# Fourth layer of a graph network: gathered rows in one ring of two chunks, refilled four tiles at a time

## The chip, the cores and the metric

One core of one Trainium2 chip. The time is that of one launch of the whole kernel on the device, in microseconds (us), median over runs. TensorE (PE) multiplies matrices, VectorE (DVE) and ScalarE (ACT) work on elements, GpSimd (POOL) here mostly issues DMAs whose addresses come from an index list, SyncE (SP) issues the other DMAs.

## The reference, cut to what matters

12 500 nodes with 32 features each, 400 000 edges sorted by destination. Four layers, each `x = x + layer(relu(layernorm(x)))`. The change is in the fourth:

```python
# edge_sh = edge_attr_4 (E, 4), edge_scalars = edge_attr_8 (E, 8); E = 400000, MUL = 8
h = relu(edge_scalars @ (fc_w1 / sqrt(8))) * SQRT2               # (E, 256)
w = (h @ (fc_w2 / sqrt(256))).reshape(E, 4, MUL, MUL)            # weights of each edge
x = node_features[edge_src]                                      # one gathered row of 32 an edge
s1, v1 = x[:, :MUL], x[:, MUL:].reshape(E, MUL, 3)
s2, v2 = edge_sh[:, 0], edge_sh[:, 1:4]
out_s = A_SCALAR * (einsum('eu,euw->ew', s1 * s2[:, None], w[:, 0])
                    + INV_SQRT3 * einsum('eui,ei,euw->ew', v1, v2, w[:, 1]))
out_v = A_VECTOR * INV_SQRT3 * (einsum('eu,euw,ei->ewi', s1, w[:, 2], v2)
                                + einsum('eui,euw->ewi', v1 * s2[:, None, None], w[:, 3]))
node_out = segment_sum(concatenate([out_s, out_v.reshape(E, 24)], axis=1), edge_dst, num_segments=N)
return node_out / sqrt(E / N)
```

The first layer gathers rows, adds edge features and sums by destination; the second is another product with weights made from edge features, the third a sum with weights from degrees. All three also gather rows by POOL's DMAs, and the change does not touch them.

## The kernel before

Edges are cut into tiles of 128 (one edge a partition), 3125 real ones, and tiles into chunks of `CT` = 16; there are `NW` = 196 chunks, and the last has 5 real tiles. A group is `G` = 4 tiles, so a chunk has four groups, called A, B, C and D here.

The fourth layer's loop is `edges3`. Its steps for a chunk `c`:

- `fetch(c)`: SP loads edge places, `edge_attr_4` and the bf16 inputs of the hidden layer. Source indices of all edges are resident in SBUF (`src_all`).
- `gather(c)`: sixteen indirect DMAs issued by POOL (L1274), one a tile; each brings 128 rows of 32 floats from the node table in HBM into one slice of the tile `hs`, 128 x 16 x 32 floats (2 KB a partition). `rows_for` clears what the last chunk leaves empty and gives the tiles to gather.
- `hidden(c, m, h)`: two matmuls into PSUM (L1285) and a ReLU on ACT (L1287) that writes a quarter of `hid`. `m` is the half of the 256 hidden values, `h` the half of the edges.
- `scalars(c)`: DVE makes the small factors `q` (L1293 and L1297, over `dd`, L1295) and `vv` (L1299) from the whole `hs`.
- `product(c, g)`: for a group's four tiles, eight fp32 matmuls (sixteen records of L1310) put `hid` times the second weight matrix into the PSUM tile `ps_w`; then DVE multiplies out `pa` (L1314, with `q`), `ps` (L1316, with eight columns of `hs`) and `pv` (L1318, with `vv`). L1316 is the last reader of these four tiles of `hs`.
- `outputs(c)`: DVE reduces `pa`, `pv` and `ps` and adds them up to `f`. `thirds` splits `f` into bf16 parts, `places` makes the 0/1 matrix of destinations on ACT (L1340), `collect` sums by destination with 16 matmuls (L1346), `add` folds the parts and sends the sum off.

Order: the program order below, per engine; a tile framework puts in the semaphore waits from what each instruction reads and writes. An iteration of the loop takes the products of chunk `c`, the outputs of chunk `c - 1` and the hidden layer and scalars of chunk `c + 1`. Loads are issued for `c + 4`, gathers for `c + 2`. On POOL nothing but gathers is queued in this layer, so how far POOL really runs ahead is set by the four buffers of the pool `gather3`: gathers of chunk `c + 4` need the buffer of chunk `c`, and wait for the last `ps` that reads it.

```python
for c in range(NW + 1):
    ...
    if c + 2 < NW:
        gather(cs[c + 2])
    for s in range(4):
        if now:
            product(now, s)
            places(now, 4 * s, 4 * s + 4)
        ...
```

Buffers of the layer: loads 6, `hs` 4, work tiles 2 (`hid`, `q`, `vv`, `pa`, `ps`, `pv` among them), `ps_h` 1, `ps_w` 2.

Of the kernel before, what the change touches and what calls it, by code (L numbers as in the profile page):

```python
# [8 lines left out]
F32 = mybir.dt.float32  # L9
# [7 lines left out]
P = 128  # L17
D = 32
NP = 125
G = 4  # L20
# [36 lines left out]
class GNN:  # L57
# [1194 lines left out]
    def edges3(self):  # L1252

        nc, tc, CT = self.nc, self.tc, self.CT
        with ExitStack() as ctx:
            ld = ctx.enter_context(tc.tile_pool(name="load3", bufs=6))
            gp = ctx.enter_context(tc.tile_pool(name="gather3", bufs=4))
            wp = ctx.enter_context(tc.tile_pool(name="work3", bufs=2))
            ph = ctx.enter_context(tc.tile_pool(name="ph3", bufs=1, space=PSUM))
            pw = ctx.enter_context(tc.tile_pool(name="pw3", bufs=2, space=PSUM))  # L1260
            ps = ctx.enter_context(tc.tile_pool(name="ps3", bufs=1, space=PSUM))

            def fetch(c):
                row = c["no"]
                c["src"] = self.sources_of(c)
                c.update(self.places_of(ld, row))
                c["sh"] = self.load(ld, "edge_attr_4", c["col"])
                c["emb"] = ld.tile([72, Q4 * B], BF16, name="emb")
                nc.sync.dma_start(c["emb"], self.emb8[:, :, ds(row, 1), :].rearrange("k f o e -> (k f) (o e)"))

            def gather(c):
                c["hs"] = gp.tile([P, CT, D], F32, name="hs")
                for k in self.rows_for(c["hs"], CT, c, 0):
                    nc.gpsimd.indirect_dma_start(  # L1274
                        out=c["hs"][:, k, :], out_offset=None, in_=self.feats[3][:],
                        in_offset=bass.IndirectOffsetOnAxis(ap=c["src"][:, k : k + 1], axis=0))

            def hidden(c, m, h):

                if (m, h) == (0, 0):  # L1280
                    c["hid"] = wp.tile([P, 2, CT, Q4, 32], F32, name="hid")
                t = ph.tile([P, 2, B], F32, name="ps_h")
                for q in range(2):
                    e0 = (2 * h + q) * B
                    nc.tensor.matmul(t[:, q, :], lhsT=self.w1s[:, m * P : (m + 1) * P],  # L1285
                                     rhs=c["emb"][:, e0 : e0 + B], start=True, stop=True)
                nc.scalar.activation(c["hid"][:, m, :, 2 * h : 2 * h + 2, :].rearrange("p b q s -> p q b s"),  # L1287
                                     t.rearrange("p q (b s) -> p q b s", s=32), AF.Relu)
# [12 lines left out]
            def product(c, g):  # L1301

                if g == 0:
                    c["pa"] = wp.tile([P, CT, 8, 16], F32, name="pa")
                    c["ps"] = wp.tile([P, CT, 8, 8], F32, name="ps")
                    c["pv"] = wp.tile([P, CT, 3, 64], F32, name="pv")
                w = pw.tile([P, 4, 256], F32, name="ps_w")
                for k in range(4):
                    for m in range(2):
                        nc.tensor.matmul(w[:, k, :], lhsT=c["hid"][:, m, 4 * g + k].rearrange("p q s -> p (q s)"), rhs=self.w2b[:, m, :],  # L1310
                                         start=m == 0, stop=m == 1)
                gs = slice(4 * g, 4 * g + 4)
                hs = c["hs"][:, gs, :]
                nc.vector.tensor_mul(c["pa"][:, gs], w[:, :, 0:128].rearrange("p g (w u) -> p g w u", u=16),  # L1314
                                     c["q"][:, gs, None, :].to_broadcast([P, 4, 8, 16]))
                nc.vector.tensor_mul(c["ps"][:, gs], w[:, :, 128:192].rearrange("p g (w u) -> p g w u", u=8),  # L1316
                                     hs[:, :, None, 0:8].to_broadcast([P, 4, 8, 8]))
                nc.vector.tensor_mul(c["pv"][:, gs].rearrange("p g i (w u) -> p (g i) w u", u=8),  # L1318
                                     w[:, :, None, 192:256].to_broadcast([P, 4, 3, 64]),
                                     c["vv"][:, gs].rearrange("p g i u -> p (g i) u")[:, :, None, :].to_broadcast([P, 12, 8, 8]))  # L1320

            def outputs(c):
                sh = c["sh"]
                f = c["f"] = wp.tile([P, CT, D], F32, name="f")
                fv = f[:, :, 8:32]
                nc.vector.tensor_reduce(f[:, :, 0:8], c["pa"], AX.X, ALU.add)
                nc.vector.tensor_reduce(fv.rearrange("p g (w i) -> p g i w", i=3),  # L1327
                                        c["pv"].rearrange("p g i (w u) -> p (g i) w u", u=8), AX.X, ALU.add)
                rs = wp.tile([P, CT, 8], F32, name="rs", bufs=1)
                nc.vector.tensor_reduce(rs, c["ps"], AX.X, ALU.add)  # L1330
                t1 = wp.tile([P, CT, 8, 3], F32, name="t1", bufs=1)
                nc.vector.tensor_mul(t1, rs[:, :, :, None].to_broadcast([P, CT, 8, 3]),
                                     sh[:, :, None, 1:4].to_broadcast([P, CT, 8, 3]))
                nc.vector.tensor_add(fv, fv, t1.rearrange("p g w i -> p g (w i)"))

            def places(c, k0, k1):
                if k0 == 0:
                    c["oh"] = wp.tile([P, CT, P], BF16, name="oh")
                for k in range(k0, k1):
                    nc.scalar.activation(c["oh"][:, k, :], self.iota, AF.Square, bias=c["local"][:, k : k + 1], scale=-1.0)  # L1340
                nc.scalar.activation(c["oh"][:, k0:k1, :], c["oh"][:, k0:k1, :], AF.Relu, bias=self.one, scale=-2.0)

            def collect(c):
                c["sum"] = ps.tile([P, B], F32, name="ps_sum")
                for k in range(CT):
                    nc.tensor.matmul(c["sum"][: 3 * D, 0:P], lhsT=c["f3"][:, k].rearrange("p i f -> p (i f)"), rhs=c["oh"][:, k, :],  # L1346
                                     start=k == 0, stop=k == CT - 1)
                c["s4"] = wp.tile([3 * D, P], F32, name="s4")
                nc.scalar.copy(c["s4"], c["sum"][: 3 * D, 0:P])

            def add(c):
                nc.tensor.matmul(c["sum"][:, P : P + D], lhsT=c["s4"], rhs=self.fold[: 3 * D], start=True, stop=True)
                s = wp.tile([P, D], F32, name="wsum", bufs=4)
                nc.scalar.copy(s, c["sum"][:, P : P + D])
                self.put_late(3, c, s)

            NW = self.NW
            cs = [{"no": c, "col": c * CT} for c in range(NW)]
            for c in range(4):
                fetch(cs[c])  # L1360
            for c in range(2):
                gather(cs[c])
            for s in range(4):
                hidden(cs[0], s % 2, s // 2)
            scalars(cs[0])
            for c in range(NW + 1):
                now = cs[c] if c < NW else None
                if c + 4 < NW:
                    fetch(cs[c + 4])
                if c + 2 < NW:  # L1370
                    gather(cs[c + 2])
                for s in range(4):
                    if now:
                        product(now, s)
                        places(now, 4 * s, 4 * s + 4)
                    if c:
                        last = cs[c - 1]
                        if s == 0:
                            outputs(last)
                            self.thirds(wp, last, 0)  # L1380
                        elif s == 1:
                            self.thirds(wp, last, 1)
                            self.thirds(wp, last, 2)
                        elif s == 2:
                            self.thirds(wp, last, 3)
                            collect(last)
                        else:
                            add(last)
                    if c + 1 < NW:
                        hidden(cs[c + 1], s % 2, s // 2)  # L1390
                        if s == 3:
                            scalars(cs[c + 1])
# [156 lines left out]
```

## Time and profile before

| | us |
|---|---|
| median of 3 runs (lowest to highest) | 20942.01 (20928.03 to 20964.97) |
| the profiled execution: its time | 20931.77 |
| its span in the trace | 20930.0 |
| busy in the span: PE, DVE, ACT, POOL | 12599.4, 12740.1, 6408.9, 14745.9 |
| fourth layer: start of the first gather | 15396.3 |
| fourth layer: start of the last gather | 20767.0 |

The profile is one execution. "L1274" is line 1274 of the kernel. A group of instructions is shown with its count, busy time and the mean time of one, and then the idle time of its engine just before them with what ended most of it ("<-"): another engine's instruction, a DMA, "issue" (nothing that the profile shows), or "remote" (a queue that the profile cannot name). The granted TensorE clock is a share of full speed. Where the span is cut into 40 slices, each digit is a busy share in tenths; the fourth layer is about the last eleven slices:

```profile
PE   2443433334766666666666666666637777777776
DVE  3554444334766666666666666666746666666666
POOL 5777777774788888888888888888755555555553
PEclk9999999998777777777777777777768888888888
```

### The profile page before, as it was taken

How to read it: one execution, taken by the hardware profiler on the slowest of the kernel's cores; microseconds unless marked ns; L12 is line 12 of the kernel's file. 1: busy time of each engine (PE TensorE's matmuls, PEld its weight loads, DVE VectorE, ACT ScalarE, POOL GpSimd, SP SyncE). 2: the span in 40 equal slices, each digit the busy share in tenths (PEclk: the TensorE clock that was granted, in tenths of full speed). 3: DMA queues.
4: the chain of work that ended last, by engine and by line, in shares of the span. 5: the costliest groups of instructions: out<-in, count | busy, mean ns of one | idle time of the engine just before them, and what ended most of it. 6: DMA issues, size and time to landing. Idle time of an engine off the chain costs nothing.

```text
span 20930.0 us, 189759 instructions
## 1 busy us (share of the span) xinstructions
PE 12599.4 (60%) x56444; PEld 6767.2 (32%) x56444; DVE 12740.1 (61%) x25505; ACT 6408.9 (31%) x13844; POOL 14745.9 (70%) x12508
## 2 busy tenths in 40 slices
PE   2443433334766666666666666666637777777776
PEld 2333433331211111111111111111125555555554
DVE  3554444334766666666666666666746666666666
ACT  0001110002333333333333333333324444444444
POOL 5777777774788888888888888888755555555553
PEclk9999999998777777777777777777768888888888
DMA  2113332112444444444444444444411111111111
GB/s 96 46 45 111 113 91 74 23 23 72 98 89 90 88 91 90 89 89 90 90 90 90 90 90 90 90 90 90 92 39 23 23 23 23 23 23 23 23 23 30
DMA packets 1482594, 1406.96 MB, mean 67 GB/s; under 512 B 1055751, under 2 KB 1250897, under 8 KB 1426409
## 3 DMA queue, kind: packets, MB, share of 16 engines
q1 hardware_dynamic: 668550, 1143.45, 17.2%
q0 software_dynamic: 750000, 205.60, 12.0%
q10 hardware_dynamic: 62992, 45.63, 0.7%
q8 instruction: 448, 7.34, 0.1%
q14 instruction: 604, 4.94, 0.1%
HBM read 1156.82 MB, written 236.20 MB: 67 GB/s over the span
## 4 chain that ended last, share of the span: by engine, by line
DVE 27%; issue 20%; PE 15%; POOL 14%; another core or an unknown queue 13%; ACT 7%; DMA 4%; DVEq 0%; ACTq 0%; SPq 0%; POOLq 0%
DVE z L853 6%; POOL acc L1008 5%; POOL hs L809 5%; PE ps_w L1310 5%; POOL hs L535 4%; PE ps_y L850 4%; DVE pv L1318 1%; DMA hs<-feat,src_all 1%; PE ps_o L860 1%; ACT oh L1340 1%; DVE f L1327 1%; DVE pa L1314 1%; ACT X L834 1%; PE ps_sum L1346 1%
## 5 line engine op out<-in xcount | busy, mean ns | idle before, releaser
L1008 POOL DMA_INDIRECT acc<-summed,rows x3125 | 5141.5, 1645 | 999.8 <-issue 882.0
L1274 POOL DMA_INDIRECT hs<-feat,src_all x3125 | 3017.6, 966 | 2462.6 <-DVE ps L1316 1460.3
L535 POOL DMA_INDIRECT hs<-feat,src_all x3125 | 3375.3, 1080 | 1368.4 <-issue 864.4
L809 POOL DMA_INDIRECT hs<-feat,src x3125 | 3210.6, 1027 | 1190.2 <-issue 944.4
L1310 PE MATMUL ps_w<-w2b,hid 128*128 128x256 f32 x12544 | 3194.7, 411 | 68.8 <-issue 53.4
L853 DVE TENSOR_TENSOR z<-ps_y,hid 128x1024 f32<-128x1024 f32 x2352 | 2837.7, 1214 | 411.2 <-PE ps_y L850 161.2
L850 PE MATMUL ps_y<-X,w2t 64*128 64x512 f32 x4704 | 2380.0, 744 | 1132.0 <-DVE z L853 656.2
L1310 PEld LDWEIGHTS ps_w<-w2b,hid 128*128 128x128 f32 x12544 | 2577.7, 209 | 625.8 <-issue 85.8
L850 PE MATMUL ps_y<-Q,w2t 64*128 64x512 f32 x4704 | 1677.6, 838 | 1678.1 <-DVE z L853 1163.8
L460 PE MATMUL ps_win<-m,oh 128*128 128x32 f32 x6272 | 1472.7, 400 | 854.9 <-ACT m L664 211.4
L472 ACT CAST f<-f 128x512 bf16<-128x512 f32 x784 | 481.2, 614 | 4785.3 <-DVE f L878 3878.6
L860 PE MATMUL ps_o<-z,sums 128*32 128x512 f32 x9408 | 1746.1, 700 | 30.0 <-DVE r L865 21.4
L460 PEld LDWEIGHTS ps_win<-m,oh 128*128 128x128 f32 x6272 | 1396.3, 328 | 927.7 <-issue 528.3
L690 PE MATMUL ps_deg<-olo,ohi 128*125 128x100 bf16 x3136 | 462.8, 298 | 2001.6 <-DVE olo L687 1416.9
L1287 ACT ACTIVATE hid<-ps_h 128x1024 f32<-128x1024 f32 x784 | 802.0, 1023 | 2368.0 <-remote 1923.5
L1314 DVE TENSOR_TENSOR pa<-ps_w,q 128x512 f32<-128x512 f32 x784 | 540.1, 689 | 1605.5 <-remote 1407.0
L824 DVE STREAM_TRANSPOSE X<-hs 128x512 f32<-128x512 f32 x392 | 273.4, 700 | 1999.8 <-DMA hs<-feat,src 1328.8
L850 PEld LDWEIGHTS ps_y<-Q,w2t 64*128 64x128 f32 x4704 | 521.2, 256 | 2923.8 <-DVE z L853 1578.9
L850 PEld LDWEIGHTS ps_y<-X,w2t 64*128 64x128 f32 x4704 | 614.2, 210 | 2343.2 <-DVE z L853 1159.5
L663 DVE TENSOR_TENSOR m<-hs,edge_attr 128x128 f32<-128x128 f32 x784 | 228.3, 291 | 1609.6 <-issue 779.8
L664 ACT ACTIVATE m<-m 128x128 f32<-128x128 f32 x784 | 240.3, 310 | 3145.1 <-DVE m L663 1175.9
L690 PEld LDWEIGHTS <-ohi 128*125 128x125 bf16 x3136 | 445.7, 215 | 1990.8 <-DVE ohi L687 1035.7
(207 smaller groups left out, 19667.1 us busy)
## 6 DMA issues: line engine op xcount, KB each, us to landing
has<-loc_t SPq DMA_DIRECT2D x392, 1024.0 KB
srow<-in_src_t SPq DMA_DIRECT2D x392, 512.0 KB
N<-n_t SPq DMA_DIRECT2D x3136, 32.0 KB
hs<-feat,src_all POOLq DMA_INDIRECT x6250
emb<-pp SPq DMA_DIRECT2D x252, 280.0 KB
emb<-emb SPq DMA_DIRECT2D x196, 360.0 KB
emb<-pp SPq DMA_DIRECT2D x252, 224.0 KB
emb<-emb SPq DMA_DIRECT2D x196, 288.0 KB
```

The costliest lines, as they stand in the source:

```text
L460: nc.tensor.matmul(c["sum"], lhsT=oh[:, k, :], rhs=feat[:, k, :], start=t0 + k == 0, stop=t0 + k == self.CT - 1)
L535: self.nc.gpsimd.indirect_dma_start(out=t[:, k, :], out_offset=None, in_=self.feats[l][:], in_offset=bass.IndirectOffsetOnAxis(ap=idx[:, t ...
L690: nc.tensor.matmul(c["deg"][:NP, :J], lhsT=ohi[:, k, :], rhs=olo[:, k, :], start=t0 + k == 0, stop=t0 + k == self.CT - 1)
L809: nc.gpsimd.indirect_dma_start(out=c["hs"][:, k, :], out_offset=None, in_=self.feats[1][:], in_offset=bass.IndirectOffsetOnAxis(ap=c["src" ...
L850: nc.tensor.matmul(y[:, q, :], lhsT=self.w2t[64 * q : 64 * q + 64, h, j, :], rhs=c["Q" if j < 3 else "X"][64 * q : 64 * q + 64, h, :], sta ...
L853: nc.vector.tensor_mul(z, y, c["hid"][:, 2 * h : 2 * h + 2, :])
L860: nc.tensor.matmul(c["o", j // 3][32 * q : 32 * q + 32, :], lhsT=self.sums[:, j, :], rhs=c["z", j, q % 2][:, q // 2, :], start=j % 3 == 0, ...
L1008: nc.gpsimd.indirect_dma_start(out=self.tabs[2][k % NTAB][:], out_offset=bass.IndirectOffsetOnAxis(ap=c["rows"][:, G * g + k : G * g + k + ...
L1274: nc.gpsimd.indirect_dma_start(out=c["hs"][:, k, :], out_offset=None, in_=self.feats[3][:], in_offset=bass.IndirectOffsetOnAxis(ap=c["src" ...
L1287: nc.scalar.activation(c["hid"][:, m, :, 2 * h : 2 * h + 2, :].rearrange("p b q s -> p q b s"), t.rearrange("p q (b s) -> p q b s", s=32), ...
L1310: nc.tensor.matmul(w[:, k, :], lhsT=c["hid"][:, m, 4 * g + k].rearrange("p q s -> p (q s)"), rhs=self.w2b[:, m, :], start=m == 0, stop=m == 1)
L1314: nc.vector.tensor_mul(c["pa"][:, gs], w[:, :, 0:128].rearrange("p g (w u) -> p g w u", u=16), c["q"][:, gs, None, :].to_broadcast([P, 4, ...
```

## The change

`hs` is no longer a tile per chunk from a pool of four, but one half of a single tile `ring` with room for two chunks; chunk `c` uses half `c % 2`. `gather(c, g)` fetches the four tiles of one group. In the loop the four gathers for group `s` of chunk `c + 2` are issued after `product(c, s)`, and they write the four tiles that the `ps` of this product has read; before, all sixteen stood ahead of the four products. At the layer's start the gathers of chunks 0 and 1 are issued in full, as before. The ring takes 4 KB a partition, where the four buffers took 8 KB.

```diff
-            gp = ctx.enter_context(tc.tile_pool(name="gather3", bufs=4))
+            gp = ctx.enter_context(tc.tile_pool(name="gather3", bufs=1))
             wp = ctx.enter_context(tc.tile_pool(name="work3", bufs=2))
+            ring = gp.tile([P, 2 * CT, D], F32, name="hs")
...
-            def gather(c):
-                c["hs"] = gp.tile([P, CT, D], F32, name="hs")
-                for k in self.rows_for(c["hs"], CT, c, 0):
+            def gather(c, g):
+                c["hs"] = ring[:, c["no"] % 2 * CT : (c["no"] % 2 + 1) * CT, :]
+                for k in self.rows_for(c["hs"][:, G * g : G * g + G], G, c, G * g):
+                    k += G * g
                     nc.gpsimd.indirect_dma_start(
                         out=c["hs"][:, k, :], out_offset=None, in_=self.feats[3][:],
                         in_offset=bass.IndirectOffsetOnAxis(ap=c["src"][:, k : k + 1], axis=0))
...
             for c in range(2):
-                gather(cs[c])
+                for s in range(4):
+                    gather(cs[c], s)
...
-                if c + 2 < NW:
-                    gather(cs[c + 2])
                 for s in range(4):
                     if now:
                         product(now, s)
+                    if c + 2 < NW:
+                        gather(cs[c + 2], s)
+                    if now:
                         places(now, 4 * s, 4 * s + 4)
```

## The prediction

> **What bounds the kernel now.** I read the page's chain and costliest groups first. They point to no single engine in the fourth layer, so I went on to the waits of that layer's middle (17500 to 20000), then to the timeline of two chunks and of the layer's start, and last to the tail, where gathers have ended and the other work still runs.
>
> Groups on the page: after the operation, busy time and mean ns of one, then the idle time before them and what ended most of it.
> ```profile
> L1274 POOL DMA_INDIRECT hs<-feat,src_all x3125 | 3017.6, 966 | 2462.6 <-DVE ps L1316 1460.3
> L1287 ACT ACTIVATE hid<-ps_h 128x1024 f32<-128x1024 f32 x784 | 802.0, 1023 | 2368.0 <-remote 1923.5
> L1314 DVE TENSOR_TENSOR pa<-ps_w,q 128x512 f32<-128x512 f32 x784 | 540.1, 689 | 1605.5 <-remote 1407.0
> ```
> The waits between 17500 and 20000:
> ```profile
> engine line waited for: us in total, times, longest us
> POOL hs L1274 <- DVE ps L1316: 687.3, 90, 11.2
> DVE pa L1314 <- remote: 686.3, 116, 10.2
> POOL hs L1274 <- issue: 414.2, 1359, 0.3
> ```
> In these 2500 us 1449 gathers run, which is 90.6 chunks of 16: 27.6 us a chunk. POOL is busy 16 x 0.966 = 15.4 of it, spends 414.2/90.6 = 4.6 between gathers, and waits 687.3/90.6 = 7.6 for the product `ps` that frees a buffer. So sixteen gathers in a row take 20.0 us (1.25 each, four take 5.0), and the 7.6 us are what a better order could win. They mirror DVE's wait before `pa`, whose releaser the profile can't name ("remote").
>
> The timeline of one chunk (start, duration, engine, operation, and in brackets what it waited for):
> ```profile
> 18031.18 0.95 POOL L1274 DMA_INDIRECT hs<-feat,src_all  x1 [7.91 <-DVE ps L1316]
> ...
> 18040.04 3.72 PE L1310 MATMUL ps_w<-w2b,hid 128*128 128x256 f32 x16 [0.54 <-issue]
> ...
> 18050.13 0.95 POOL L1274 DMA_INDIRECT hs<-feat,src_all  x1 [0.30 <-issue]
> ...
> 18054.02 0.69 DVE L1314 TENSOR_TENSOR pa<-ps_w,q 128x512 f32<-128x512 f32 x1 [9.35 <-remote]
> 18054.06 1.02 ACT L1287 ACTIVATE hid<-ps_h 128x1024 f32<-128x1024 f32 x1 [10.19 <-remote]
> ...
> 18058.38 0.94 POOL L1274 DMA_INDIRECT hs<-feat,src_all  x1 [7.30 <-DVE ps L1316]
> ```
> A run of sixteen gathers goes from 18031.18 to 51.08. TensorE's matmuls of a group ran from 18040.04 to 43.76, but DVE's `pa`, which waits for them, and ACT's `hid`, which reads other results of TensorE, restart together at 18054, 2.9 us after the run's last gather. I call this the hold: inside a long run of gathers DVE and ACT learn of TensorE's work late. Early in a run (up to some 7 us after its first gather) they still learn of it within 0.4 to 0.7 us. POOL's next run in turn waits for the group that was held. So run and hold take turns, and that makes the chunk.
>
> Windows of two chunks each, with gathers and in the tail without (busy us and count of each engine, granted TensorE clock, DMA share, GB/s):
> ```profile
> core 0: us, PE busy (x) PEld busy (x) DVE busy (x) ACT busy (x) POOL busy (x), PEclk, DMA share, GB/s
> 18003.08:18058.12 55.04, 39.53 (x183) 31.27 (x182) 35.62 (x47) 25.50 (x56) 30.68 (x32) 0.84 0.12 23
> 20780.50:20816.60 36.10, 34.44 (x182) 27.55 (x180) 35.57 (x49) 25.58 (x57) 0.00 (x0) 1.00 0.01 2
> ```
> DVE does the same 35.6 us in both, so without gathers the chunk is 18.05 us and DVE is full; with them 27.5. The clock explains little (39.53 of PE work still fits 55.04). DVE's own pitch in the tail, from one `ps` to the next, is 8.5 us from a chunk's last group D to the next chunk's first, A (20780.16 to 20788.69: `scalars` and `outputs` lie between), then 3.4, 2.9 and 3.5.
>
> **The change part by part.**
>
> *Nothing is added to the count.* Still 3125 gathers, the same products. `rows_for` clears four tiles at a time, so the part-filled last chunk takes two more memsets: some 0.7 us at 0.35 each, once; nothing. The ring is half as large. Each gather of four waits for one `ps`; extra semaphore instructions on POOL take 17 ns each: 3 more a chunk, 0.05 us, nothing.
>
> *Is order kept by slices of the one ring tile?* Today gathers into one `hs` tile start 1.25 us apart, while data of a gather needs longer: chunk 0's last gather starts at 15415.14 and the `q` that waits for it at 15417.92, 2.8 us later. So gathers into one tile don't wait for each other; I take slices as kept apart in the ring too. If not, see the rivals.
>
> *The start.* Today's four buffers let 64 gathers run without a break, 80 us, and the second group's `pa` is held for it:
> ```profile
> 15474.22 0.69 DVE L1314 TENSOR_TENSOR pa<-ps_w,q 128x512 f32<-128x512 f32 x1 [34.43 <-remote]
> ```
> After: 32 gathers, then four more on the first group's `ps`; 36 x 1.25 = 45.0 us from 15396.3 gives 15441.4, and 2.9 of hold 15444.3. Gain 30 us, once.
>
> *The steady chunk.* What the four gathers wait for is moved from chunk c-2's group D (by the four buffers POOL runs four chunks ahead) to each group's own `ps`. On POOL only later gathers are queued behind that wait; `q` needs their data one chunk on, some 25 us (today three), against 2.8 for one gather's data, so the shorter lead is free. I walk POOL against the tail's DVE pitch, with t = 0 at the `ps` of group C, POOL having been idle. C's four gathers: 0 to 5.0. D's `ps` at 3.5, gathers 5.0 to 10.0. A's `ps` at 3.5 + 8.5 = 12.0: POOL idle 2.0, gathers 12.0 to 17.0. B's `ps` at 15.4, gathers 17.0 to 22.0. Next C: by DVE alone 18.3, which would make the chunk 22.0, but its matmuls end about 17 to 18, inside the run. If held as today to 2.9 us past the run's end, its `ps` comes at 22.0 + 2.9 + 0.69 + 0.42 = 26.0. Bounds for the chunk: 22.0 if the 2.0 us pause lets POOL's backlog, whatever it is, empty (results early in a run are prompt), 26.0 if not. The pause is 2.0 against the 2.9 that today's hold outlasts a run, so I take the nearer end, 25.5. That saves 27.6 - 25.5 = 2.1 us on some 190 chunks: 400 us. Next late then is still the hold, no engine.
>
> Sum: 20931.8 - 30 - 400 = 20502 profiled; the median of the runs stands 10 above the profiled execution (20942.0 against 20931.8), so 20 510.
>
> Two chunks' work takes 55.04 us beside gathers and 36.10 without. A rule speaks against reading this as I do: the Trainium skill's page "SBUF — State Buffer", section "Who interferes with whom", has PE and ACT waiting on nobody and DMA not contending with compute engines. By it gathers would not delay TensorE's results, and where they are placed would be worth 0: 20 940. The rows decide for me.
>
> **The rivals.**
>
> *Placing is worth nothing.* If only the count of gathers matters, two holds a chunk (20.0 + 2 x 4.0 = 28.0, hold and two DVE steps each) take the place of the one of 7.6: 20 900 (the start alone) to 20 990 (28.0). For it: the same sixteen gathers a chunk run beside the same products. Against: the 7 us of promptness.
>
> *The pauses don't add up, they repeat (slower).* The walk has two runs of ten microseconds a chunk. If each holds the group behind it until 2.9 + 1.1 = 4.0 us after its end (D at the first, C at the second), and DVE's long D-to-A step comes on top, uncovered by 1 to 3.5 us, the chunk is 29.0 to 31.5: (1.4 to 3.9) x 190 less 30 = 21 170 to 21 640. It decides from 7.6 us of POOL idle a chunk upwards. For it: today one hold a chunk covers DVE's long step; four dependences give POOL no slack to run through it. Against: in 5 us runs the readers were prompt. Whole-tile ordering, instead of by slices, would be further out (each group then pays 5.0 + 2.8), but the start's rows speak against it.
>
> *The hold vanishes (much faster).* If runs of ten microseconds are short enough throughout, the chunk is 22.0: 5.6 x 190 + 30 = 1094, 19 850. POOL's own 20.0 us is the floor.
>
> **How the numbers follow.** The walk with a partial hold (20 300 to 20 650 by itself: 24.4 to 26.2 a chunk) 0.43; hold gone 0.15; placing worth nothing 0.11; slower 0.31. A measurement of this kernel can tell about 0.2%, 42 us. So faster 0.43 + 0.15 = 0.58, same 0.11, slower 0.31. The range goes from 20 000, which keeps a part of the vanished hold (22.7 a chunk), to 21 350, the lower half of the slower case.
>
> **What would show it.** Right: POOL's wait for `ps` falls from 7.6 to about 5.5 us a chunk and is split in two (some 2 before A's gathers, 3 to 4 before C's); DVE's "remote" wait before `pa` falls by as much; the second group's `pa` comes near 15444; DVE's busy time is unchanged. Wrong: POOL waits four times a chunk, or DVE's waits before `pa` come after each run of four; or `q` waits for gathered data, which would mean that two chunks of lead are too few.

## The result, and the profile after

The change makes the kernel slower: 21 423.91 us (median of 4 runs, 21 410.75 to 21 425.35) against 20 935.02 (4 runs, 20 921.05 to 20 964.97). The ratio is 1.023, with a 95% interval of 1.0212 to 1.0248. The prediction was 20 510, so it has the wrong sign.

The span of the changed kernel is 21421.1 us. Two lines are added above the loop's steps, so that line 1274 of before is now 1276, 1314 is 1316, 1316 is 1318, and so on. The groups on its page that answer to those of before (ACT's `hid` is no longer among those listed):

```profile
L1276 POOL DMA_INDIRECT hs<-feat,src_all x3125 | 3079.9, 986 | 2921.7 <-DVE ps L1318 1886.6
L1316 DVE TENSOR_TENSOR pa<-ps_w,q 128x512 f32<-128x512 f32 x784 | 542.3, 692 | 2286.5 <-PE ps_w L1312 1390.9
```

Gathers and `pa` cost per piece what they did. The idle time before them grew, and what ends most of DVE's is no longer the "remote" that cannot be named but TensorE's product itself. The waits between 17500 and 20000:

```profile
engine line waited for: us in total, times, longest us
ACT s L1351 <- remote: 1151.6, 82, 15.0
...
PE ps_sum L1354 <- ACT s L1351: 845.9, 75, 12.4
POOL hs L1276 <- DVE ps L1318: 801.7, 92, 11.0
DVE pa L1316 <- PE ps_w L1312: 594.0, 140, 9.9
```

In this window 1324 gathers run, 82.75 chunks, so a chunk takes 30.2 us where it took 27.6. POOL is busy 15.8 us of it, spends 4.2 between gathers, and waits 801.7/82.75 = 9.7 for a `ps`, where it waited 7.6. (30.2 - 27.6) x 190 = 494 us; the medians differ by 489. So the steady chunk accounts for the loss.

The two lines about `s` are new among the long waits. `s` is ACT's copy of the sums that `collect` has made on TensorE, and the fold matmul of `add` (L1354) reads that copy. The timeline from the end of one run of gathers to the start of the next shows what hangs on it:

```profile
18028.64 0.95 POOL L1276 DMA_INDIRECT hs<-feat,src_all  x1 [0.30 <-issue]
18032.10 0.26 ACT L1351 COPY s<-ps_sum 96x128 f32<-96x128 f32 x1 [14.85 <-remote]
...
18032.41 0.63 PE L1354 MATMUL ps_sum<-fold,s 96*128 96x32 f32 x2 [11.95 <-ACT s L1351]
18032.56 1.01 ACT L1289 ACTIVATE hid<-ps_h 128x1024 f32<-128x1024 f32 x1
...
18032.85 5.78 PE L1312 MATMUL ps_w<-w2b,hid 128*128 128x256 f32 x18
...
18038.67 0.69 DVE L1316 TENSOR_TENSOR pa<-ps_w,q 128x512 f32<-128x512 f32 x1 [8.20 <-PE ps_w L1312]
...
18039.28 0.41 DVE L1318 TENSOR_TENSOR ps<-ps_w,hs 128x256 f32<-128x256 f32 x1
...
18039.96 0.95 POOL L1276 DMA_INDIRECT hs<-feat,src_all  x1 [10.37 <-DVE ps L1318]
```

The last gather of a run ends at 18029.59. TensorE's sums, held inside the run, reach ACT 2.5 us later (the hold of the prediction). On TensorE's queue stands the fold, which needs this copy, and behind it product A; product A also needs the last quarter of `hid`, which ACT makes only after the copy. So the sum goes: 2.5 hold, 0.3 copy, 0.5 to the product's first matmul, 5.8 for its row of matmuls, 1.3 for `pa`, `ps` and the handing over: the 10.4 us that POOL waits. Then all sixteen gathers follow without a break, because B, C and D are done before POOL gets to them: the four waits of a chunk are one. So it goes in about two chunks of three; in the others POOL waits a second time, 1 to 4 us, ahead of group D's gathers.

The matmuls of product A are slow as well: 5.8 us for the 18 records of that row, where the 16 of a group take 3.6 to 3.7 elsewhere. Windows of the changed kernel (busy us and count of PE, PEld, DVE, ACT and POOL, then the granted TensorE clock):

```profile
core 0: us, PE busy (x) PEld busy (x) DVE busy (x) ACT busy (x) POOL busy (x), PEclk, DMA share, GB/s
18047.00:18050.00 3.00, 3.00 (x20) 2.60 (x19) 2.26 (x5) 0.98 (x2) 2.39 (x3) 1.00 0.09 12
...
18053.00:18056.00 3.00, 0.00 (x0) 0.00 (x0) 3.00 (x6) 0.00 (x0) 2.39 (x3) 0.54 0.10 14
18056.00:18059.00 3.00, 0.00 (x0) 0.00 (x0) 3.00 (x2) 0.00 (x0) 2.39 (x3) 0.50 0.11 13
...
18064.00:18066.00 2.00, 2.00 (x6) 1.55 (x6) 0.00 (x0) 1.88 (x7) 0.00 (x0) 0.50 0.48 137
```

TensorE is idle from 18051.2 on, waiting for `s`; its clock is granted at 0.50 by 18056 and is still 0.50 when the next product A runs. Two records take 0.43 us elsewhere (16 in 3.62, 14 in 3.19), so 18 would take 4.05, and some 5.8 - 4.05 = 1.7 us of the wait are the clock's. The Trainium skill's page "TensorE: Matmul & The Clock Gate", section "Part 1: The HAM clock gate", has the clock halved after an idle window of some 3.4 us. The windows here show the halving, but sooner after the last matmul: the 0.54 from 18053 to 18056 puts it near 18053.2 (an estimate), 2 us after.

### The profile page after: what moved, and what is told of

The parts are those of the page before. It is cut to its first block, busy times and chain, and to the rows that moved or that the text cites. A ratio compares the mean times of both kernels' runs of the same rounds, so it can differ in the third digit from the quotient of the medians.

```text
span 21421.1 us, 190342 instructions
## 1 busy us (share of the span) xinstructions
PE 12486.4 (58%) x56444; PEld 6756.7 (32%) x56444; DVE 12803.7 (60%) x25507; ACT 6384.9 (30%) x13844; POOL 14787.4 (69%) x12508
## 4 chain that ended last, share of the span: by engine, by line
DVE 20%; PE 19%; another core or an unknown queue 19%; issue 18%; POOL 14%; ACT 6%; DMA 4%; DVEq 0%; ACTq 0%; SPq 0%; POOLq 0%
PE ps_w L1312 9%; DVE z L853 6%; POOL hs L809 5%; POOL acc L1008 5%; PE ps_y L850 4%; POOL hs L535 4%; DMA hs<-feat,src_all 1%; PE ps_o L860 1%; ACT X L834 1%; PE ps_h L1287 1%; DVE cnt L990 1%; DVE eq L985 1%; DVE X L824 1%; PE ps_win L460 1%
## 5 line engine op out<-in xcount | busy, mean ns | idle before, releaser
L1312 PEld LDWEIGHTS ps_w<-w2b,hid 128*128 128x128 f32 x12544 | 2636.2, 212 | 495.1 <-issue 11.6
L1354 PE MATMUL ps_sum<-fold,s 96*128 96x32 f32 x392 | 123.5, 408 | 2150.3 <-ACT s L1351 1937.8
L1342 ACT ACTIVATE oh<-iota,local 128x128 bf16<-128x128 f32 x3136 | 1056.9, 391 | 48.7 <-DMA edge_attr<-in_edge_attr 25.9
```

## The experiments

Runs went to several chips, and the kernel before was run on each. On three of them it took 20 777 to 20 935 us; on two it took 18 934 and 18 979, and no profile taken there (none is of the kernel before) shows TensorE's results held. Each run is therefore told beside before on its own chip, and I call the chips those with and those without holds. Also, the tile framework does not only put in waits: it reorders each engine's queue. Where a built program's order undid an edit, this is said.

### Lead, place of issue, or slices?

Three edits of the ring, and one that gives it up. With a ring of four chunks (with holds; before 20 793.20):

```diff
-            ring = gp.tile([P, 2 * CT, D], F32, name="hs")
+            ring = gp.tile([P, 4 * CT, D], F32, name="hs")
...
-                c["hs"] = ring[:, c["no"] % 2 * CT : (c["no"] % 2 + 1) * CT, :]
+                c["hs"] = ring[:, c["no"] % 4 * CT : (c["no"] % 4 + 1) * CT, :]
...
-            for c in range(2):
+            for c in range(4):
...
-                    if c + 2 < NW:
-                        gather(cs[c + 2], s)
+                    if c + 4 < NW:
+                        gather(cs[c + 4], s)
```

> The changed kernel with a ring of four chunks: gathers for chunk c + 4 overwrite, four at a time, what the products of chunk c have read; the lead is four chunks again, as before. Theory A (the order costs: a chunk's gathers now begin on the product of its group A, which waits on TensorE's queue behind results held to the end of the run before): the lead doesn't matter, 21 400 to 21 460, 30.2 us a chunk, POOL idle 9.7 a chunk. Rival B (two chunks of lead are too few): back to 20 930 to 20 980.

21 450.41 us. Twice the lead changes nothing; rival B is out.

All sixteen gathers issued after product D (same chip):

```diff
-                    if c + 2 < NW:
-                        gather(cs[c + 2], s)
+                    if c + 2 < NW and s == 3:
+                        for g in range(4):
+                            gather(cs[c + 2], g)
```

> The changed kernel's ring of two chunks, but all sixteen gathers for chunk c + 2 issued after the product of group D of chunk c, as one run that waits for D alone, as the runs of before did. Theory A: 20 900 to 20 980, 27.6 us a chunk. Rival B (the lead): 21 400 or more.

21 448.87 us: theory A's number was missed. Its wait between 17500 and 19900 shows why:

```profile
POOL hs L1276 <- DVE ps L1318: 804.5, 78, 10.9
```

That is 10.3 us a chunk, where the changed kernel waits 9.7 and the kernel before 7.6, and the runs still begin on group A's `ps`. Nothing but gathers is queued on POOL, so where they stand in the program doesn't matter; each waits only for the reader of its own slice. The theory had to be made sharper: the ring lets a run begin on A instead of D. Two runs on another chip with holds (before 20 935.04) test that.

```diff
-            gp = ctx.enter_context(tc.tile_pool(name="gather3", bufs=1))
+            gp = ctx.enter_context(tc.tile_pool(name="gather3", bufs=2))
...
-            ring = gp.tile([P, 2 * CT, D], F32, name="hs")
...
-                c["hs"] = ring[:, c["no"] % 2 * CT : (c["no"] % 2 + 1) * CT, :]
+                if g == 0:
+                    c["hs"] = gp.tile([P, CT, D], F32, name="hs")
...
-                    if c + 2 < NW:
-                        gather(cs[c + 2], s)
+                    if c + 2 < NW and s == 3:
+                        for g in (0, 1, 2, 3):
+                            gather(cs[c + 2], g)
```

> Two tiles from a pool instead of two halves of one ring; all sixteen gathers for chunk c + 2 are issued after product D of chunk c. A tile of a pool comes free as a whole, after the last reader of it, group D's ps. Theory A, made sharper by the two ring runs (what matters is neither lead nor the place of the issue, but that slices of a ring come free one by one, so that a run starts on group A's ps instead of D's): within 0.4% of before, POOL idle 7 to 8 us a chunk. Rival B (lead of two chunks, or where the gathers are issued): 3% above before, like the ring runs.

20 903.39 us, 0.2% below before. The waits between 17500 and 20000 are those of before again (687.3 and 686.3 there):

```profile
POOL hs L1276 <- DVE ps L1318: 696.7, 90, 11.0
...
DVE pa L1316 <- remote: 677.1, 112, 10.0
```

Two buffers, a lead of two chunks, and the time of before: what costs is the release slice by slice, not the lead.

The other edit kept the ring and put group D's gathers first:

```diff
-                    if c + 2 < NW:
-                        gather(cs[c + 2], s)
+                    if c + 2 < NW and s == 3:
+                        for g in (3, 0, 1, 2):
+                            gather(cs[c + 2], g)
```

> The ring of two chunks by slices, gathers issued after product D, but group D's four gathers first, then A, B, C. POOL takes them in order, so the run starts on D's ps and the other slices are free by then. Theory A: within 0.4% of before. Rival (a ring tile as such costs, in semaphores or in its place in SBUF): 3% above before.

21 455.02 us, a miss that tells little: in its trace the runs still begin on group A's `ps`, as in the ring with all sixteen issued after product D (at 18019.51, after 10.36 us of idle; the other three groups of that chunk follow within the run). The framework seems to have sorted the groups back, so a ring whose runs begin on D was not tried, and that a ring as such costs something is not excluded by a run.

### What stands behind the held result

The hidden step goes ahead of each product and `add` two groups later (with holds; first before 20 793.20, then timed against 20 777.38):

```diff
                 for s in range(4):
+                    if c + 1 < NW:
+                        hidden(cs[c + 1], s % 2, s // 2)
                     if now:
                         product(now, s)
...
-                        else:
-                            add(last)
-                    if c + 1 < NW:
-                        hidden(cs[c + 1], s % 2, s // 2)
-                        if s == 3:
-                            scalars(cs[c + 1])
+                    if s == 1 and c > 1:
+                        add(cs[c - 2])
+                    if c + 1 < NW and s == 3:
+                        scalars(cs[c + 1])
+            add(cs[NW - 1])
```

> The changed kernel; the hidden layer's step for the next chunk stands ahead of each product instead of behind it, and add (the fold matmul behind ACT's copy of the collected sums) comes two groups later, after the next chunk's product B. So on TensorE product A no longer stands behind the fold nor behind a hidden step of the held stretch. Theory A: of POOL's idle 10.4 us the ACT copy (0.26), the fold (0.63) and product A's matmuls (5.8) go from the path, 6.7 us in about two chunks of three: 25 to 26.5 us a chunk, 20 450 to 20 750. Rival C (the hold itself, not what stands behind it, sets the chunk: another result is held as long): within 100 us of 21 420.

20 341.17 us, 5% below the changed kernel and 109 us below theory A's range. The timeline between two runs:

```profile
18022.37 0.94 POOL L1276 DMA_INDIRECT hs<-feat,src_all  x1 [0.30 <-issue]
18025.51 0.69 DVE L1316 TENSOR_TENSOR pa<-ps_w,q 128x512 f32<-128x512 f32 x1 [7.15 <-remote]
...
18026.12 0.41 DVE L1318 TENSOR_TENSOR ps<-ps_w,hs 128x256 f32<-128x256 f32 x1
...
18026.80 0.95 POOL L1276 DMA_INDIRECT hs<-feat,src_all  x1 [3.49 <-DVE ps L1318]
```

The hold is still there (`pa` starts 2.2 us past the run's end), but product A's matmuls are done by then: `pa` follows at once, and POOL waits 3.5 us instead of 10.4. With about 1.7 more before B's gathers, that makes 24.9 us a chunk.

> early_both again, timed against before. In the last four runs the kernel before took 18 979 us instead of 20 790 to 20 940, and the page of no kernel there shows a wait on results of TensorE that came late. Theory A with holds on this chip (before at 20 800 or more): 2 to 3% below before. Without holds on this chip (before near 18 980): POOL's sixteen gathers of 20 us bound every version, within 0.3% of before.

20 360.89 us (4 runs) against 20 777.38 (7 runs): 0.9798, interval 0.9782 to 0.9815. With holds this version beats both kernels.

The same edit on the kernel before, whose runs begin on D (before 20 935.04 on that chip):

> The kernel before (four tiles, runs that start on D's ps), with the hidden step ahead of each product and add two groups later, as in early_both. Theory A (the gain of early_both was TensorE's chain of copy, fold and product A behind the hold; before's idle of 7.3 us holds no such chain, but a product that was held and the next one behind it): little, 0 to 1.5% below before. Rival C (early steps help whatever the run's start is): as fast as early_both, 2% or more below before.

21 725.38 us, 3.8% slower: both expectations missed. Its timeline:

```profile
18011.06 1.02 ACT L1287 ACTIVATE hid<-ps_h 128x1024 f32<-128x1024 f32 x1 [11.10 <-remote]
...
18012.13 1.01 PE L1285 MATMUL ps_h<-emb,w1s 72*128 72x512 bf16 x2 [11.53 <-ACT hid L1287]
...
18012.94 6.01 PE L1310 MATMUL ps_w<-w2b,hid 128*128 128x256 f32 x16
...
18018.99 0.69 DVE L1314 TENSOR_TENSOR pa<-ps_w,q 128x512 f32<-128x512 f32 x1 [2.57 <-PE ps_w L1310]
18019.60 0.41 DVE L1316 TENSOR_TENSOR ps<-ps_w,hs 128x256 f32<-128x256 f32 x1
...
18020.28 0.94 POOL L1274 DMA_INDIRECT hs<-feat,src_all  x1 [12.41 <-DVE ps L1316]
```

Now the hidden step stands ahead of product D on TensorE; it waits for ACT's `hid`, which is held, to free the one `ps_h`, and D's matmuls (6.0 us) wait behind it. D is what these runs begin on. One edit thus gains 5% where a run begins on A and loses 4% where it begins on D. That fits theory A in its general form: POOL's wait is the hold plus the work that stands between the held result and the `ps` that frees the next slice.

The halves of the edit, `add` alone and the hidden step alone (diffs as above, one hunk each). Their first runs fell on a chip without holds (before 18 978.82):

> One half of early_both: the changed kernel with only add (the fold matmul) two groups later. Theory A (product A stands behind two held results, the last hidden step's and the collected sums'; each alone keeps it behind the run): only copy and fold go from the path, 0.3 + 0.6 us a chunk, 21 230 to 21 430. Rival D (the fold alone is what holds product A): 20 340 to 20 600, like early_both.

> The other half: the changed kernel with only the hidden step ahead of each product. Theory A: the fold, behind ACT's copy of the held sums, still stands ahead of product A on TensorE: 21 200 to 21 430. Rival D (the hidden step alone holds product A): 20 340 to 20 600.

18 988.05 and 18 986.13 us, each within 0.05% of before: nothing told apart there. Then `add` alone with holds (before 20 777.38), beside the changed kernel itself on the same chip:

> late_add once more, since its first run saw no holds. With holds, theory A (the last hidden step's result keeps product A behind the run as well): 21 230 to 21 430. Rival D (the fold alone kept it): 20 340 to 20 600. Without holds: near 18 980, and nothing told apart.

> The changed kernel itself beside before. Theory A, that the change's cost lies in what stands behind a held result and in nothing else: 2 to 3% above before if before shows 20 800 or more; within 0.3% of before if before is near 18 980. Rival F (part of the cost is there without holds): slower than before by 1% or more on either.

21 428.74 and 21 427.35 us: `add` alone gains nothing, as theory A has it, but the test is weak. In its timeline the fold still comes after only the first two matmul records of product A; the framework had moved it forward. The changed kernel is 3.1% above before on this chip. The hidden step alone was tried once more and fell on the other chip without holds (before 18 933.70):

> early_hidden once more, since its first run saw no holds. With holds, theory A (the fold, behind ACT's copy of the held sums, still stands ahead of product A): 21 200 to 21 430. Rival D (the last hidden step alone kept product A behind the run): 20 340 to 20 600. Without holds: near 18 980.

18 901.89 us, 0.2% below before. So which of the two things is needed to free product A, or whether both are, stays open.

### What holds the results

Half of the gathers left out (with holds, before 20 793.20), and SyncE issuing plain DMAs of the same shape in place of POOL's gathers (with holds, before 20 935.04):

```diff
+            nc.vector.memset(ring, 0.0)
...
+                    if k > 1:
+                        continue
                     k += G * g
```

> The changed kernel without two of each group's four gathers (the other rows stay zero); the products are all computed. Theory A (results are held while a run of gathers lasts and for some 2.5 us after it): runs are at most 10 us, the chunk falls by more than the 10 us of POOL's own work once the held result isn't the last of the chunk: 18.5 to 20.5 us, 19 200 to 19 600. Rival C (a hold of fixed length each chunk, whatever the run): 30.2 less 10 at most, and no lower than 22: 19 900 to 20 400.

```diff
-                    nc.gpsimd.indirect_dma_start(
-                        out=c["hs"][:, k, :], out_offset=None, in_=self.feats[3][:],
-                        in_offset=bass.IndirectOffsetOnAxis(ap=c["src"][:, k : k + 1], axis=0))
+                    nc.sync.dma_start(c["hs"][:, k, :], self.feats[3][ds(P * ((16 * c["no"] + k) % 96), P), :])
```

> The changed kernel with its gathers replaced by plain DMAs issued by SyncE, of the same shape (128 rows of 128 bytes into the same slices) but of consecutive rows, so other data. Theory P (results of TensorE are held by POOL's making of gathers, not by the transfers): no hold, 17.8 to 19 us a chunk as in half_gathers, 18 950 to 19 250. Theory T (the small transfers hold them, whoever issues them): 20 800 or more.

18 981.46 and 19 061.79 us. The window 16500 to 18500 of each, half the gathers first:

```profile
16500.00:18500.00 2000.00, 1939.56 (x10109) 1540.98 (x10108) 1979.61 (x2580) 1433.75 (x3152) 953.12 (x897) 1.00 0.12 28
```

```profile
16500.00:18500.00 2000.00, 1877.75 (x9929) 1539.18 (x9929) 1952.00 (x2535) 1390.47 (x3096) 0.00 (x0) 1.00 0.18 35
```

DVE is full (1980 and 1952 of 2000 us) and the clock is 1.00. In the first, 897 gathers of 8 a chunk make 17.8 us a chunk. Twelve microseconds went for ten of POOL's work, as theory A has it, and the time is below its range. The second moves the same 51.4 MB without POOL, in more and smaller packets (450 000 for 100 000), 18.1 us a chunk by its DVE instructions (17.8 x 2580/2535), and nothing is held: small transfers as such don't hold TensorE's results. Its rows are consecutive and come by another queue, so by itself it doesn't tell POOL's making of the gathers from the gathered rows. The pauses that follow do: they leave the gathers as they are and only break POOL's run of them.

Pauses on POOL ahead of each four gathers:

```diff
+            idle = gp.tile([P, 1024], F32, name="idle")
...
+                nc.gpsimd.memset(idle, 0.0)
+                nc.gpsimd.tensor_copy(c["hs"][:, G * g : G * g + 1, :], idle[:, None, 0:D])
                 for k in self.rows_for(c["hs"][:, G * g : G * g + G], G, c, G * g):
```

> The changed kernel with a pause of some 1.2 to 1.5 us on POOL ahead of each four gathers (a memset of 1024 floats a partition into a scratch tile, and a copy of 32 of them into the group's first rows, which the gathers then overwrite). POOL's own work rises from 20.0 to some 25.5 us a chunk. Theory A (only long unbroken runs of gathers hold results; two runs of two or four gathers never did): holds vanish, POOL waits almost nothing, 25.5 us a chunk, 20 450 to 20 650 in all, PE's clock back near 1.00. Rival E (any dense stretch of POOL work holds them, pauses or not): the run is 5 us longer and held to its end, 34 to 36 us a chunk, 22 200 to 22 500.

> paced once more. Its first run, without holds, took 24.5 us a chunk, all of it POOL's. With holds, theory A (unbroken runs of gathers hold results, a pause of 1.3 us every four ends it): 19 900 to 20 400. Rival E (pauses change nothing, the longer run is held to its end): 22 000 or more.

19 899.01 us without holds (before 18 978.82) and 20 360.81 with (before 20 777.38, the changed kernel 21 427.35). From the first gather to the last the fourth layer took 4882 us in the one and 4872 in the other: with pauses the two kinds of chip are alike there, and the 462 us between the totals lie ahead of the layer, whose first gather starts 471 us later. POOL's longest entries between 17500 and 19500, with holds:

```profile
POOL hs L1279 <- issue: 316.9, 1192, 0.3
POOL hs L1279 <- DVE f L476: 7.3, 24, 0.3
```

No long wait for `ps` is left (1.2 us in all). A pause of 1.2 us (0.98 for the memset, 0.21 for the copy) every four gathers ends the hold, and POOL may be busy in it. The same sixteen gathers then take 24.9 us a chunk, less than the 30.2 of the changed kernel, so gathered rows don't hold results either unless POOL makes them in a long run. Rival E is out.

> early_both with the same pauses. Theory A: POOL's work of some 25.5 us a chunk is the bound, nothing held: 20 400 to 20 550, no better than early_both alone (20 341), because the pause costs what the hold did. Rival E: 21 200 or more.

19 859.88 us on the chip without holds, near paced (19 899.01): POOL is the bound. With holds it wasn't run. A shorter pause (memset of 128 floats a partition) went to the other chip without holds:

> paced with a shorter pause: the memset clears 128 floats a partition instead of 1024, so the pause ahead of each four gathers should be some 0.4 us instead of 1.2, and POOL's work some 21.7 us a chunk instead of 24.4. Theory A, if any break of POOL's gathers ends the hold: 196 x 21.7 = 4250 us for the layer, 19 700 to 19 850 in all, 4.5 to 5.5% below before. Rival G (the pause must be long enough for what is held to be let through): holds as in the changed kernel, 21 400 or more. Where nothing is held: 19 230 to 19 330 against 18 980.

19 257.28 us against 18 933.70, 1.0169 (1.0152 to 1.0186): there it costs what its POOL time costs. Whether it would end holds stays open.

### Where nothing is held

The chain of the page, share of the span by engine: the changed kernel on a chip with holds (changed_again), then late_add on one without.

```profile
issue 17%; DVE 16%; another core or an unknown queue 15%; PE 12%; POOL 11%; ACT 5%; DMA 2%; SPq 1%; DVEq 0%; ACTq 0%; POOLq 0%
```

```profile
POOL 35%; DVE 14%; issue 11%; DMA 9%; PE 5%; ACT 1%; DVEq 0%; another core or an unknown queue 0%; POOLq 0%; SPq 0%; ACTq 0%
```

The entry that the profile cannot name goes from 15% to 0, and POOL leads the chain. late_add and early_hidden have the change's ring and its grouped gathers, and took within 0.2% of before there; 1562 gathers in 2000 us of late_add are 20.5 us a chunk, POOL's own sixteen gathers and little else. The changed kernel itself was not run on such a chip, so that it costs nothing there is an inference from these two.

## Why the prediction was wrong

**Counts and durations: right.** 3125 gathers at 986 ns against 966, DVE's busy time 12803.7 against 12740.1.

**The start: right.** The second group's `pa` comes 50.8 us after the layer's first gather (15393.05), where it came 78.0 after it: 27 us gained for 30 predicted. The run was of 36 gathers, as predicted, and ended at 15438.1; the hold after it was 5.7 us and not 2.9.

```profile
15443.81 0.69 DVE L1316 TENSOR_TENSOR pa<-ps_w,q 128x512 f32<-128x512 f32 x1 [7.27 <-remote]
```

**Slices: right, and the heart of the matter.** Gathers do wait slice by slice; two_tiles shows that without it the time of before is back. I took it as something that could only free slices sooner. **The lead: right.** Four chunks or two make no difference (21 450.41 and 21 448.87).

**The hold: right in kind.** That long runs of gathers delay TensorE's results, and not the transfers or the clock alone, is what by_sync, half_gathers and paced_again show together. So it was on three of the five chips that the experiments ran on. What I drew from the rule of the Trainium skill's page "SBUF — State Buffer", section "Who interferes with whom", that gathers would not delay TensorE's results, fits the two chips without holds (chain entry 0%, 20.5 us a chunk) and not the three with (by_sync's 18.1 us a chunk against the changed kernel's 30.2). The rule itself is about access to SBUF, and no run here shows whether a hold has to do with that.

**The steady chunk: wrong, at one step.** It is "A's `ps` at 3.5 + 8.5 = 12.0". The 8.5 us are DVE's pitch from D to A in the tail, where no gathers run and TensorE is ahead of DVE. I walked DVE's pitch and let the hold strike only at C. I did not walk TensorE's own queue: between the products D and A stand `collect`, the last hidden step and the fold, three steps with two handings over from TensorE to ACT and back, and with the gathers running they fall into the held stretch. So A's `ps` came 23.4 us after C's (18015.89 to 18039.28), and not 12.0: D's came 6.9 after C's for 3.5, held inside the run, and A's 16.5 after D's for 8.5. That is 9.7 us after the run's last gather (18029.59), where I had 2.0. The clock, which I took to explain little, is 1.7 us of that wait. The idle time is 9.7 us a chunk for 5.5 predicted, the chunk 30.2 for 25.5: (30.2 - 25.5) x 190 = 893 us, nearly all of the 914 between 20 510 and 21 424.

**The rivals.** "The pauses repeat" gave 21 170 to 21 640 and the right threshold (idle above 7.6 us a chunk). Its number holds the time, but by luck, for its mechanism did not come: not two holds of 4.0 us and a rest, one for each run of ten microseconds, but in most chunks one run of sixteen gathers and one wait of 10.4. "Placing is worth nothing" is out with holds by early_both, and seems right without them. "The hold vanishes" did not happen by the change, but paced_again shows what it would take.

## What to carry to other kernels

When a buffer is released by slices instead of as a whole, ask which reader the next writer now starts on, and then walk every engine's queue up to that reader, not the busiest engine's pitch: here the earliest slice freed was the one behind the longest chain. A release that comes sooner is no gain where it only moves the same work to a worse phase. And compare before and after on more than one chip before trusting a gain of 2%: the same pair can differ by 3% on one chip and, it seems, by nothing on the next.

## What the runs showed of the hardware

While POOL made gathers for longer than some 7 to 10 us without a break, TensorE's results reached DVE and ACT late. Up to 7 us into a run of the kernel before they came within 0.4 to 0.7 us; 10 us into it, ACT's `hid` started 1.8 us after its matmuls (18039.51 to 18041.29). Some came through late but inside the run: group D's `pa` at 18022.16, 3.0 us after its matmuls, and in the layer's first run of 64 gathers the second group's, for which DVE waited 34.43 us, 2.2 us before that run's end. The rest came after the run, 2.2 to 2.9 us in the steady chunks shown and 5.7 after the changed kernel's first run. Ends of matmuls are modelled in these traces, so whether the matmuls finish late or only the word of them comes late isn't told apart. Runs of two to four gathers (half_gathers) or pauses of 1.2 us every four (paced_again) did away with it. It shows on three of the five chips; on the other two the kernel before, the same program, is 9% faster (18 934 and 18 979 us against 20 777 to 20 935), of which, as an estimate from late_add's 20.5 us a chunk, 196 x (27.6 - 20.5) = 1390 us are the fourth layer's; some 500 lie ahead of it (471 between the two paced runs). What differs between the chips, and by what path a gather holds up TensorE, no run here shows.
